# A 5x5 convolution inside a four-layer network on one Trainium2 core: shared sums seeded by a copy in PSUM instead of by identity products

## The chip, the cores and the metric

The kernel runs on one core of one Trainium2 chip, all in float32. The metric is the device time of one execution in microseconds (us). Before the change it is 4425.42 us, the median of three runs (4424.64 to 4433.18). The engines are named as in the profile: PE (TensorE, matrix products; PEld is its weight load), DVE (VectorE), ACT (ScalarE), POOL (GpSimd) and SP (SyncE, which issues DMAs).

## The reference, cut to what matters

Four images `x[4, 128, 64, 64]` go through four residual layers, each fed by a group norm. Layer 1 is the one that the change touches:

```python
x = x + attention(_gn(x))                              # layer 0, 4096 x 4096 scores per image
x = x + conv5x5(_gn(x), c)                             # layer 1: c[128, 128, 5, 5], padding 2
x = x + project(selective_scan(expand(_gn(x))))        # layer 2: two directions, 64 states
x = x + conv3x3(_gn(x), main_w)                        # layer 3
```

The convolution takes five kernel rows w0 to w4. For a pair of output rows, with image rows x0 to x5 above each other, the kernel writes

    even row = [(w1+w2)x2 + (w3+w4)x4] + w0 x0 + w1(x1-x2) + w3(x3-x4)
    odd row  = [(w1+w2)x2 + (w3+w4)x4] + w0 x1 + w2(x3-x2) + w4(x5-x4)

so that the bracket is computed once for both. Each term is five products, one for each kernel column. In the code `SUM12` and `SUM34` are w1+w2 and w3+w4, and `diff` holds the differences of rows.

## The kernel before

**Two streams.** `scan_core` (L1190) is layer 2's scan. It is written as 1024 ticks, 256 per image. A tick is one product `db` on POOL (`drive`, L1255), exponentials `da` on ACT (`decay`, L1240), the scan itself on DVE (`recur`, L1260, line L1268), a product with `cr` on DVE (L1271) or on POOL (`weigh`, L1286, line L1289), and every fourth tick a group of sums `y` on PE (`collect`, L1291, line L1309). Everything else of all images (attention, convolutions, operands of the next scan) is a second stream, `images()`, written as one generator that yields a cost in us after each piece it has issued. The loop at the end of `program` mixes them: after each half tick it adds `pace / 2` to a credit and pulls pieces from the generator until the credit is used up. `PACE` (2.8) is the credit per tick while images 0 to 2 are scanned, `ENDPACE` (1.5) while image 3 is. `PRODUCT` (0.86) is the charge for one matrix product of 512 columns, `HOP` (1.7) and `SLOT` (0.7) are charges for steps that put little on PE. This mixing fixes the order of instructions in every engine's queue; each engine then works through its queue in order.

**Stages.** While image b is scanned, the second stream does the attention of image b+1 (`attention`, L437: scores L482, exponentials L488, values L494), then its 5x5 convolution (`conv_pairs`, L830), then the operands of its scan (`scan_prep`, L1006). `before(b)` (in `program`) lets a scan begin when its operands are there; if they are not, it pulls pieces without any tick beside them. Attention keeps a second bank for scores, so the scan's `da` tiles are 512 wide; during a convolution, and all through the last image's scan, `widen` makes them 1024 wide ("wide").

**The 5x5 convolution of images 1 to 3** (`lean`) works on pairs of output rows, one even and one odd, in four chunks of 16 rows. For a chunk it makes three sums in three PSUM banks:

- `pq` in bank `s`: 10 products, the part that the two rows of each pair have in common;
- `pe0` in bank `a`: 15 products, the even rows' own part;
- `pe1` in bank `z`: 15 products, the odd rows' own part.

ACT copies `pq` to an SBUF tile `q` (L977). Then one more product with the identity matrix adds `q` to `pe0`, and another adds it to `pe1` (L991). `add` (L930) lets DVE add each finished sum to the image `xs` (L932), and ACT squares the result for the next group norm (L331). A finished sum's reader is issued late, after the third product of the following sum, so that PE's queue runs ahead. The first image has another form (`wide` weights, no identity products).

```python
if lean:
    nc.tensor.matmul(acc, ident, qs, start=False, stop=True)   # L991
    yield PRODUCT
```

Of the kernel before, what the change touches and what calls it, by code (L numbers as in the profile page):

```python
# [35 lines left out]
CH = 1024  # L36
# [6 lines left out]

PRODUCT, HOP, SLOT, PACE, ENDPACE, AHEAD = 0.86, 1.7, 0.7, 2.8, 1.5, 4


BQ, BK, BX, BP, CONVB, BD, DSKIP, MAINB, CONVW, ALOG = 0, 1, 2, 3, 4, 5, 6, 7, 8, 12
# [3 lines left out]
def conv_preact_kernel(  # L53
# [16 lines left out]
    nc = tc.nc  # L70
    B, C, H, W = x.shape
    L = H * W
# [21 lines left out]
    def bank(tag, name):  # L94
        return pools.get(tag, ps).tile([P, MM], F32, tag=tag, name=name)
# [20 lines left out]
    ident = const.tile([P, P], F32, name="ident")  # L116
# [19 lines left out]
    for d in range(2):  # L136
        r = slice(d * HALF, (d + 1) * HALF)
# [84 lines left out]
    SUM12, SUM34, HSUM, HDIF = 5, 6, 7, 8  # L222
# [607 lines left out]
    def conv_pairs(b, xs, tag, st, st2, lean):  # L830

        NP, CK = H // 2, CH // W // 2
# [33 lines left out]

        wide = pools.get("fill") if not lean else None
# [6 lines left out]
        def combine(j, n):  # L874
            for m, (p, q, op) in enumerate(
                ((1, 2, ALU.add), (0, 2, ALU.subtract), (3, 1, ALU.subtract))
            ):
                a, b_ = (rows[:, 2 * j + r : 2 * (j + n) + r - 1 : 2, :] for r in (p, q))
                nc.vector.tensor_tensor(views[m][0][:, j : j + n, :], a, b_, op)

        def differences(i):
            last = i == 3
            if wide:
                combine(8 * i, 8)
            odd(8 * i, 8 + last)
            even(8 * i + 1, 8 + last)
# [25 lines left out]
        def flat(t):  # L912
            return t.rearrange("p (h w) -> p h w", w=W)
# [3 lines left out]
        piece(1)  # L917
        differences(0)
        K5 = 5
        steps, done = [], None  # L920
        taps5 = more[0] if wide else exchange(b)[:, : NTAP * C].rearrange("p (k c) -> p k c", c=C)

        def matrix(w, dx):
            if w < SUM12:
                return taps5[:, w * K5 + dx, :]
            if w < HSUM:
                return cs[:, (w - SUM12) * K5 + dx, :]
            return more[1][:, w - HSUM, dx, :]

        def add(c, y, acc):  # L930
            i = 2 * c + y
            nc.vector.scalar_tensor_tensor(  # L932
                chunk(xs, c, y), flat(acc), 1.0, chunk(xs, c, y), ALU.mult, ALU.add,
                accum_out=st2.sum(i),
            )
            st2.squares(i, chunk(xs, c, y), xs[:, 0:1])

        for c in range(L // CH):
            j = c * CK
            if c < 2:  # L940
                piece(2 + c)
            if c < 3:
                differences(c + 1)
            accs = [
                (bank("s", f"pq_{b}_{c}"), ((SUM12, image, 2 * j + 2), (SUM34, image, 2 * j + 4))),
                (bank("a", f"pe0_{b}_{c}"),
                 ((0, image, 2 * j), (1, diff, j), (3, diff, j + 1))),
                (bank("z", f"pe1_{b}_{c}"),
                 ((0, image, 2 * j + 1), (2, diff, NP + j + 1), (4, diff, NP + j + 2))),
            ]  # L950
            if wide:
                total, first, last = (combo(n) for n in range(3))
                accs = [
                    (accs[0][0], (accs[0][1][1], (HSUM, total, j))),
                    (bank("y", f"pm_{b}_{c}"), ((HDIF, diff, j),)),
                    (accs[1][0], ((0, first, j), (3, diff, j + 1))),
                    (accs[2][0], ((2, last, j), (4, diff, NP + j + 2))),
                ]
            for n, (acc, parts) in enumerate(accs):
                k, total = 0, len(parts) * K5  # L960
                for w, view, r in parts:
                    for dx in range(K5):
                        k += 1
                        nc.tensor.matmul(  # L964
                            flat(acc), matrix(w, dx), view(r, dx),
                            start=k == 1, stop=k == total and (n == 0 or not lean),
                        )
                        if k == 3 and done is not None:
                            done()
                            done = None  # L970
                        if k % 3 == 0:
                            yield 3 * PRODUCT
                if n == 0:
                    qs = pools["bg"].tile([P, MM], F32, tag="w", bufs=4, name=f"q_{b}_{c}")

                    def done(acc=acc, qs=qs, c=c):
                        nc.scalar.copy(qs, acc)  # L977
                        for y in range(0 if lean else 2):
                            nc.gpsimd.tensor_tensor(
                                chunk(xs, c, y), chunk(xs, c, y), flat(qs), ALU.add  # L980
                            )
                    yield PRODUCT
                elif wide and n == 1:
                    def done(acc=acc, c=c):
                        for y, op in enumerate((ALU.subtract, ALU.add)):
                            nc.vector.tensor_tensor(
                                chunk(xs, c, y), chunk(xs, c, y), flat(acc), op
                            )
                else:
                    if lean:  # L990
                        nc.tensor.matmul(acc, ident, qs, start=False, stop=True)  # L991
                        yield PRODUCT

                    def done(acc=acc, c=c, y=n - len(accs) + 2):
                        add(c, y, acc)
        yield HOP
# [657 lines left out]
```

## Time and profile before

| what | value |
|---|---|
| median of three runs | 4425.42 us |
| span of the profiled execution | 4424.0 us |
| PE busy in it | 3917.4 us, 89% |
| DVE busy | 3698.5 us, 84% |
| POOL busy | 3602.1 us, 81% |
| ACT busy | 2358.3 us, 53% |
| products with the identity (L991) | 48 matrix instructions (24 products of two each), 25.1 us |
| copies of `pq` (L977) | 16 (4 of them for image 0), 585 ns each |

The span runs from the first to the last instruction of one profiled execution; it lies 1.4 us under the median and 0.6 us under the lowest of the three runs. A float32 product of 128x128 by 128x512 shows as two matrix instructions. A row "engine line op out<-in xcount | busy, mean ns | idle" is a group of alike instructions; the idle column is the time the engine stood still just before them. In a table by stretches each engine has its busy time and, in brackets, its number of instructions. Busy times of PE have modelled ends; the start times in the timeline are recorded.

Landmarks of the second stream in this execution, read from PE's timeline:

| image | attention, first query product to last product of its last block | 5x5 convolution, first to last product |
|---|---|---|
| 1 | 728.2 to 1375.6 | 1383.3 to 1558.7 |
| 2 | 1660.9 to 2309.4 | 2318.4 to 2493.9 |
| 3 | 2605.8 to 3249.4 | 3261.1 to 3436.3 |

### The profile page before, as it was taken

To read this page: it belongs to the slowest core of one execution; us is meant where nothing else is said; L and a number is where in the kernel's file an instruction comes from. 1 tells how busy PE (TensorE), PEld (TensorE's weight loads), DVE (VectorE), ACT (ScalarE), POOL (GpSimd) and SP (SyncE) were. 2 spreads that over 40 slices of the span, in tenths; PEclk is the share of its full clock that TensorE was granted. 3 is DMA by queue.
4 is the path that set the end of the run, shared out by engine and by line. 5 is a ranking of instruction groups with operands and counts; after the bars stand their busy time and mean duration, and the time that the engine had idled before them with its cause. 6 is when DMAs were issued, how large, how long until landed. Compare 5 with 4: busy or idle time off the path is not lost. (4 is left out here: it accounts for less than half of the span.)

```text
span 4424.0 us, 43050 instructions
## 1 busy us (share of the span) xinstructions
PE 3917.4 (89%) x13480; PEld 1485.9 (34%) x13480; DVE 3698.5 (84%) x3472; ACT 2358.3 (53%) x4269; POOL 3602.1 (81%) x1713
## 2 busy tenths in 40 slices
PE   8999997999999979999989889999989748575667
PEld 4444433333333323333333333333333212121212
DVE  4722217999999989999999889999999899999996
ACT  3333217666665376666664576666653744454533
POOL 3433307999999978999999889999989889999995
PEclk9999999999999989999999989999999869787888
DMA  1000016545455566554544564454545665656562
GB/s 64 21 1 1 0 53 228 182 170 175 168 186 180 179 214 212 177 175 174 180 164 180 205 231 177 165 179 173 180 175 182 226 228 193 232 202 235 187 226 84
DMA packets 213167, 726.06 MB, mean 164 GB/s; under 512 B 25152, under 2 KB 26432, under 8 KB 212672
## 3 DMA queue, kind: packets, MB, share of 16 engines
q1 hardware_dynamic: 211328, 722.49, 46.3%
q8 instruction: 108, 1.77, 0.2%
q14 instruction: 131, 1.07, 0.1%
q10 hardware_dynamic: 1600, 0.73, 0.1%
HBM read 653.98 MB, written 69.14 MB: 163 GB/s over the span
## 5 line engine op out<-in xcount | busy, mean ns | idle before, releaser
L1258 POOL TENSOR_TENSOR db<-dx,br 128x1024 f32<-128x1024 f32 x1024 | 2398.1, 2365 | 223.8 <-DMA dx<-dxd 55.6
L1251 ACT ACTIVATE da<-de,a_neg 128x512 f32<-128x512 f32 (+1 forms) x1640 | 1302.4, 797 | 740.6 <-DVE da L1268 300.5
L482 PE MATMUL sc<-r,x 128*128 128x512 f32 x2048 | 1078.6, 609 | 14.8 <-ACT last L1284 6.9
L494 PE MATMUL acc<-exchange,v 128*128 128x512 f32 x2048 | 1048.3, 594 | 2.3
L1289 POOL TENSOR_TENSOR hc<-hc,cr 128x1024 f32<-128x1024 f32 x386 | 913.0, 2365 | 22.5 <-ACT last L1284 19.7
L1271 DVE TENSOR_TENSOR hc<-da,cr 128x512 f32<-128x512 f32 (+1 forms) x1003 | 839.6, 837 | 65.0 <-DVE da L1268 0.5
L1268 DVE TENSOR_TENSOR_SCAN da<-da,last,db 128x512 f32<-128x512 f32 (+1 forms) x480 | 863.1, 1798 | 24.3 <-POOL db L1258 12.1
L488 ACT ACTIVATE exchange<-sc 128x512 f32<-128x512 f32 x1024 | 603.5, 589 | 510.4 <-PE sc L482 503.9
L1309 PE MATMUL y<-hc,sel 128*32 128x512 f32 x4096 | 611.9, 647 | 270.6 <-POOL hc L1289 245.3
L482 PEld LDWEIGHTS sc<-r,x 128*128 128x128 f32 x2048 | 361.3, 190 | 585.6 <-issue 379.2
L494 PEld LDWEIGHTS acc<-exchange,v 128*128 128x128 f32 x2048 | 386.4, 190 | 499.2 <-issue 478.0
L1268 DVE TENSOR_TENSOR_SCAN hc<-da,last,db 128x512 f32<-128x512 f32 (+1 forms) x288 | 490.9, 1704 | 6.5 <-ACT da L1251 5.2
L1268 DVE TENSOR_TENSOR_SCAN da<-da,da,db 128x512 f32<-128x512 f32 x365 | 469.7, 1287 | 6.2 <-ACT da L1251 5.9
L536 POOL TENSOR_TENSOR sidep<-sidep,exchange 128x512 f32<-128x512 f32 x120 | 170.7, 1422 | 273.5 <-ACT exchange L488 271.3
L1268 DVE TENSOR_TENSOR_SCAN hc<-da,hc,db 128x512 f32<-128x512 f32 x251 | 322.0, 1283 | 35.6 <-ACT da L1251 11.8
L1309 PEld LDWEIGHTS y<-hc,sel 128*32 128x32 f32 x4096 | 114.4, 113 | 706.1 <-POOL hc L1289 337.7
L536 DVE TENSOR_TENSOR sided<-sided,exchange 128x512 f32<-128x512 f32 x120 | 95.9, 799 | 221.5 <-ACT exchange L488 220.1
L1268 DVE TENSOR_TENSOR_SCAN da<-da,db 128x512 f32<-128x512 f32 (+1 forms) x158 | 232.5, 1471 | 15.5 <-POOL db L1258 7.1
L698 PE MATMUL pcm<-xpm,cs 128*128 128x512 f32 x432 | 210.1, 635 | 23.1 <-ACT xpm L387 23.1
L964 PE MATMUL pe<-df,exchange 128*128 128x512 f32 x480 | 214.2, 595 | 0.0
L516 PE MATMUL zp<-exchange,ones 128*32 128x512 f32 x1536 | 204.9, 600 | 8.3 <-DVE xs L583 8.3
L1284 ACT COPY last<-da 128x1 f32<-128x1 f32 x474 | 73.8, 156 | 254.5 <-DVE hc L1271 252.0
(241 smaller groups left out, 2839.1 us busy)
## 6 DMA issues: line engine op xcount, KB each, us to landing
br<-bm SPq DMA_DIRECT2D x512, 512.0 KB, 5.2
cr<-cm SPq DMA_DIRECT2D x512, 512.0 KB, 3.9
de<-dd SPq DMA_DIRECT2D x64, 512.0 KB, 4.7
dx<-dxd SPq DMA_DIRECT2D x64, 512.0 KB, 6.2
x<-in_x_dram SPq DMA_DIRECT2D x16, 512.0 KB, 5.9
xs<-in_x_dram SPq DMA_DIRECT2D x16, 512.0 KB, 6.1
xsd<-xs SPq DMA_DIRECT2D x16, 512.0 KB, 6.0
xcd<-xc SPq DMA_DIRECT2D x16, 512.0 KB, 2.8
```

The costliest lines, as they stand in the source:

```text
L482: nc.tensor.matmul(sc, xn[:, bass.ts(j, P)], rq[blk], start=True, stop=True)
L488: nc.scalar.activation(pt, sc, AF.Exp)
L494: nc.tensor.matmul(acc[blk], v[:, j, :], ring[:, u % NRING, :], start=j == 0, stop=j == NJT - 1)
L536: eng.tensor_tensor(s, s, ring[:, u % NRING, :], ALU.add)
L698: nc.tensor.matmul(acc.rearrange("p (r w) -> p r w", w=W), weights[:, t, :], xp[:, y : y + RPM, dx : dx + W], start=t == 0, stop=t == k * ...
L964: nc.tensor.matmul(flat(acc), matrix(w, dx), view(r, dx), start=k == 1, stop=k == total and (n == 0 or not lean),)
L1251: nc.scalar.activation(da, rep["de", b, c, d, g][:, bass.ts(h, size)], AF.Exp, scale=a_neg[:, at(i)])
L1258: nc.gpsimd.tensor_tensor(dbs[i], rep["dx", b, c, d, g], rows["b", b, c, d, q], ALU.mult)
L1268: nc.vector.tensor_tensor_scan(h, da, db[:, cut], before, ALU.mult, ALU.add)
L1271: nc.vector.tensor_tensor(hc[:, cut], h, rows["c", b, c, d, q][:, cut], ALU.mult)
L1289: nc.gpsimd.tensor_tensor(hcs[i], hcs[i], rows["c", b, c, d, q], ALU.mult)
L1309: nc.tensor.matmul(y[r : r + SG, :], sel, hcs[first + gg][:, bass.ts(h, MM)], start=q == back, stop=False, tile_position=(0, r), skip_grou ...
```

## The change

For images 1 to 3 the common sum of a chunk goes into a bank that is `s` and `z` in turn. ACT copies it into bank `a`. The even rows' 15 products then add to that copy, and the odd rows' 15 products add to the common sum in its own bank; neither begins with `start=True`, so they add to what stands there. The tile `q` and the 24 identity products are gone. The order of a chunk's sums becomes: common sum of chunk c, odd rows of chunk c-1, even rows of chunk c. For the first chunk nothing lies between the common sum and the even rows, and a `yield HOP` stands there. `PACE` goes from 2.8 to 2.77. The charge for the identity products falls away, and with it the one `PRODUCT` that was charged after the common sum. The first image's convolution keeps its order.

```diff
-PRODUCT, HOP, SLOT, PACE, ENDPACE, AHEAD = 0.86, 1.7, 0.7, 2.8, 1.5, 4
+PRODUCT, HOP, SLOT, PACE, ENDPACE, AHEAD = 0.86, 1.7, 0.7, 2.77, 1.5, 4
...
+        def group(acc, parts, begun=False):
+            nonlocal done
+            k, of_all = 0, len(parts) * K5
+            for w, view, r in parts:
+                for dx in range(K5):
+                    k += 1
+                    nc.tensor.matmul(
+                        flat(acc), matrix(w, dx), view(r, dx),
+                        start=k == 1 and not begun, stop=k == of_all, skip_group_check=lean,
+                    )
+                    if k == 3 and done is not None:
+                        done()
+                        done = None
+                    if k % 3 == 0:
+                        yield 3 * PRODUCT
+
+        NCK, held, owns = L // CH, {}, {}
+
+        def shared_of(c):
+            j = c * CK
+            held[c] = bank("sz"[c % 2], f"pq_{b}_{c}")
+            yield from group(
+                held[c], ((SUM12, image, 2 * j + 2), (SUM34, image, 2 * j + 4))
+            )
+
+        def second_of(c):
+            nonlocal done
+            j, acc = c * CK, held.pop(c)
+            yield from group(
+                acc, ((0, image, 2 * j + 1), (2, diff, NP + j + 1), (4, diff, NP + j + 2)), True
+            )
+            done = lambda: add(c, 1, acc)
+
+        def first_of(c):
+            nonlocal done
+            j, acc = c * CK, owns.pop(c)
+            yield from group(
+                acc, ((0, image, 2 * j), (1, diff, j), (3, diff, j + 1)), True
+            )
+            done = lambda: add(c, 0, acc)
+
+        def part(c):
+            owns[c] = bank("a", f"pe0_{b}_{c}")
+            nc.scalar.copy(owns[c], held[c])
+
+        for c in range(NCK + 1 if lean else 0):
+            if c < NCK:
+                advance(c)
+                yield from shared_of(c)
+                done = lambda c=c: part(c)
+            if c > 0:
+                yield from second_of(c - 1)
+            else:
+                yield HOP
+                done()
+                done = None
+            if c < NCK:
+                yield from first_of(c)
...
-                    if lean:
-                        nc.tensor.matmul(acc, ident, qs, start=False, stop=True)
-                        yield PRODUCT
```

More of the change, by code (lines that the diff above doesn't have):

```diff
@@ L919, in conv_pairs @@
         K5 = 5
-        steps, done = [], None
+        done = None
         taps5 = more[0] if wide else exchange(b)[:, : NTAP * C].rearrange("p (k c) -> p k c", c=C)
@@ L936, in add, with advance @@
             st2.squares(i, chunk(xs, c, y), xs[:, 0:1])
-        for c in range(L // CH):
-            j = c * CK
+        def advance(c):
             if c < 2:
@@ L943, in conv_pairs @@
                 differences(c + 1)
-            accs = [
[L945 to L949, printed above, removed]
-            ]
[L951 to L958, printed above, removed]
@@ L959, in conv_pairs @@
-            for n, (acc, parts) in enumerate(accs):
[L960 to L972, printed above, removed]
+        def group(acc, parts, begun=False):
[13 more added lines that the diff above has]
+                        yield 3 * PRODUCT
@@ new lines, in first_of @@
+        def first_of(c):
[18 more added lines that the diff above has]
+                done()
+                done = None
+            if c < NCK:
+                yield from first_of(c)
@@ new lines, in conv_pairs @@
+        for c in range(0 if lean else NCK):
+            j = c * CK
+            advance(c)
+            total, first, last = (combo(n) for n in range(3))
+            accs = [
+                (bank("s", f"pq_{b}_{c}"), ((SUM34, image, 2 * j + 4), (HSUM, total, j))),
+                (bank("y", f"pm_{b}_{c}"), ((HDIF, diff, j),)),
+                (bank("a", f"pe0_{b}_{c}"), ((0, first, j), (3, diff, j + 1))),
+                (bank("z", f"pe1_{b}_{c}"), ((2, last, j), (4, diff, NP + j + 2))),
+            ]
+            for n, (acc, parts) in enumerate(accs):
+                yield from group(acc, parts)
@@ L977, in done @@
                         nc.scalar.copy(qs, acc)
-                        for y in range(0 if lean else 2):
+                        for y in range(2):
                             nc.gpsimd.tensor_tensor(
@@ L982, in conv_pairs @@
                     yield PRODUCT
-                elif wide and n == 1:
+                elif n == 1:
                     def done(acc=acc, c=c):
```

## The prediction

> **What bounds the kernel now.** I read the table by stretches first, because the share over the whole span mixes stages. Columns: stretch, its length, then busy us of PE, PEld, DVE, ACT, POOL, the granted clock, DMA share and GB/s.
>
> ```profile
> 800.00:1370.00 570.00, 561.67 (x2170) 210.87 (x2172) 541.58 (x558) 368.16 (x758) 531.77 (x230) 1.00 0.51 178
> 1700.00:2300.00 600.00, 590.71 (x2266) 219.18 (x2258) 570.34 (x586) 385.44 (x795) 561.45 (x243) 1.00 0.50 174
> 2640.00:3245.00 605.00, 599.62 (x2312) 222.37 (x2311) 576.80 (x592) 390.49 (x806) 565.91 (x245) 1.00 0.50 175
> 1396.00:1540.00 144.00, 144.00 (x449) 57.27 (x450) 135.55 (x84) 56.73 (x63) 136.75 (x62) 1.00 0.53 181
> 2330.00:2478.00 148.00, 148.00 (x472) 58.10 (x471) 137.61 (x85) 56.74 (x63) 142.06 (x64) 1.00 0.49 178
> 3273.00:3434.00 161.00, 161.00 (x513) 63.28 (x512) 150.34 (x94) 61.80 (x69) 153.19 (x69) 1.00 0.50 176
> 3600.00:4350.00 750.00, 497.48 (x1560) 148.92 (x1556) 727.87 (x430) 360.09 (x570) 724.54 (x331) 0.81 0.61 213
> ```
>
> The first three rows lie in the attentions of images 1 to 3, the next three in their 5x5 convolutions, the last in the scan of image 3. In the convolutions PE is busy all the time, at full clock, and the list of PE's waits in 1396 to 1540 is empty: there PE sets the pace, with DVE and POOL at 93 to 96%. In the attentions PE is at 98.7% (1752.0 of 1775 us), DVE at 95.1%, POOL at 93.5%: three engines near their limit. At the end PE has a third of its time free, and DVE and POOL set the pace.
>
> The same table for the products `db` alone counts ticks, one each: 164, 174 and 175 in the attentions, 44, 45 and 49 in the convolutions, 235 in the last stretch. So a tick takes 1775/513 = 3.46 us in an attention, 453/138 = 3.28 in a convolution, 750/235 = 3.19 at the end.
>
> Then PE's timeline of the convolution (start, length, with modelled end, so I use starts):
>
> ```profile
> 1409.83 1.92 PE L1309 MATMUL y<-hc,sel 128*32 128x512 f32 x16
> 1411.68 1.12 PE L991 MATMUL pe<-q,ident 128*128 128x512 f32 x2
> 1412.64 4.50 PE L964 MATMUL pe<-xpe,exchange 128*128 128x512 f32 x10
> 1416.98 6.17 PE L964 MATMUL pe<-df,exchange 128*128 128x512 f32 x14
> 1423.08 1.92 PE L1309 MATMUL y<-hc,sel 128*32 128x512 f32 x16
> 1424.93 2.84 PE L964 MATMUL pe<-df,exchange 128*128 128x512 f32 x6
> 1427.62 1.02 PE L991 MATMUL pe<-q,ident 128*128 128x512 f32 x2
> 1428.47 4.06 PE L964 MATMUL pq<-xpe,cs 128*128 128x512 f32 x9
> ```
>
> An identity product holds PE's queue for 1428.47 - 1427.62 = 0.85 us (0.96 right after sums `y`). Sums `y` of four ticks hold it for 1.85 us, which is 0.46 us a tick, and 0.49 with the `skip` products once in 32 ticks.
>
> **The change, part by part.**
>
> *Identity products.* 2 for each of 4 chunks of 3 images, 24 x 0.855 = 20.5 us of PE, all in stretches where PE is the limit: **-20.5 us**.
>
> *Where the ticks go.* The scan has 1024 ticks before and after, and no edit takes DVE or POOL work out of a tick, so what counts is which ticks lie beside which work. The planner's credit can be followed in both sources. Attentions end at ticks 190, 444 and 700 before, and at 192, 446 and 701 after; convolutions end at 243, 497, 753 against 243, 496, 752; the operands of images 2 and 3 are finished one tick earlier. So attentions get 184 ticks each before and 186 after (+6 in all, at `PACE` 2.77 instead of 2.8), convolutions 53 each before and 51, 50, 51 after (-7), the operand stages 17, 19 and 20 both times, and the end 251 before and 252 after (+1).
>
> - A tick less in a convolution saves only its share of `y`, as PE is the limit there: 7 x 0.49 = **-3.4 us**. A convolution's products per tick rise slightly, because 39 charges now stand for 40 products of a chunk; DVE (423.5/138 = 3.07 us a tick) and POOL (3.13) stay under PE's 3.28.
> - A tick more at the end costs a whole one: **+3.2 us**.
> - A tick more in an attention, with the same attention products spread over more ticks, is the disputed cost. If PE alone set the pace there, it would cost 0.49 us; if DVE and POOL did, 3.46. Six ticks: +2.9 or +20.8 us. The waits speak for neither: in the third attention DVE waited for the exponentials and for `db` as listed below, 7.5 of 605 us, and PE's idle time there is 5.4 us.
>
> ```profile
> DVE da L1268 <- ACT da L1251: 4.9, 8, 2.2
> DVE hc L1268 <- ACT da L1251: 1.7, 4, 0.8
> DVE da L1268 <- POOL db L1258: 0.9, 3, 0.4
> ```
>
> Both engines hardly wait, so I take the middle: **+11.9 us**. I keep both ends for the range.
>
> *The copy.* 12 copies from PSUM to SBUF become 12 from PSUM to PSUM. The page's rows bracket the new form: exponentials without bias take 589 ns into SBUF (L488) and 600 into PSUM (L1127), activations with bias 686 (L1098) and 667 (L1099), and L977 itself 585. So it is 585 give or take 20 ns; ACT has over half its time free in the convolution.
>
> The Trainium skill, "ScalarE: Activation LUTs", in "Step-by-step: what each stage is for", calls ScalarE's way into PSUM faster than into SBUF; the exponential's rows here say 11 ns slower and the biased ones 19 ns faster. By either, the sum moves by less than 0.1 us.
>
> *Waits that the copy adds.* For chunks 1 to 3 the copy is issued three products into the odd rows' sum of the chunk before, and PE first needs it 12 products later: 12 x 0.86 = 10.3 us of cover. Bank `a` must also have been read by DVE, which is issued ten products before the copy. Of the 12 copies before, nine start 0.03 to 0.04 us after the last product of `pq` ends and the others 0.2, 1.8 and 2.5 us after, behind exponentials that wait for DVE. So I cost these at nothing; if the cover went, nine even-row sums would wait, with `y` queued behind them on PE and the scan's tiles behind `y`. For chunk 0 there is no cover: PE goes from the common sum to the even rows and must wait for the end of the last product (0.16 us after its slot), a hop of 0.04, the copy of 0.585 and a hop back of about 0.05, some 0.85 us. Three images: **+2.6 us**. The odd rows' sum follows 15 products after ACT has read its bank, and the banks `s` and `z` are reused 12 products after their reader is issued: nothing.
>
> *Not on the path.* SP's queue, the DMAs, POOL's instructions and DVE's additions are the same in number; `q` leaves a ring of four tiles for which nobody waits in a convolution.
>
> The Trainium skill, "PSUM — Partial Sum Buffer", in "The four PSUM rules" and its summary, speaks against the change: engine writes do not touch the bits that decide whether a product adds or overwrites, so a seed other than zero should go through PE. It also says that products add where an earlier product set the bit, which bank `a` has had since the attention. No row here shows a product adding to a copy. Kept to the letter, the rule brings 12 identity products back, 10.3 us of the 20.5.
>
> *Sum.* -20.5 - 3.4 + 2.6 + 3.2 + 11.9 = **-6.2 us**. The profiled span, 4424.0, becomes 4417.8; it lies 1.4 us under the median of 4425.4, which becomes **4419.2**. What a measurement of this kernel can tell from no change is about 0.2%, 8.85 us.
>
> **Rivals.**
>
> - *PE alone sets the pace of the attentions.* For it: PE is the busiest at 98.7%. Against it: its loads of weights and ends are modelled, and DVE waits for it little. Six ticks cost 2.9 us: -20.5 - 3.4 + 2.6 + 3.2 + 2.9 = -15.2, **4410**. This is what the lower pace is worth if it is right.
> - *DVE and POOL set it alone.* For it: DVE's waits are 1% too, and its small gaps between instructions count as idle though they can't be used. Six ticks cost 20.8: +2.7, **4428**. The gain of the convolution is given back tick by tick.
> - *The seed is late in every chunk* (the other side). Place: the even rows' first product in chunks 1 to 3, nine times. ACT's queue is in order, and a copy behind an exponential that waits for DVE (2.4 us is a usual such wait in the convolution) also delays the next exponentials. It costs from the point where a copy ends more than 10.3 us after its issue; at 2.4 us each, 9 x 2.4 = +21.6, so +15.4 on the forecast, **4441**. It makes the kernel slower by over 0.2% from 1.7 us each. Against it: the latest copy of before ended 3.1 us after its sum.
> - *The identity products are not gone, or come back as others*: excluded, the instruction order of the changed kernel has none in images 1 to 3.
>
> **How the numbers follow.** Forecast 0.40, PE alone 0.28, DVE and POOL alone 0.20, late seeds 0.08, anything else 0.04, counted as slower. The operand stages give noise: with 0.03 less credit per tick their pieces fall otherwise between ticks, and the pieces pulled without a tick before scans 1, 2 and 3 go from 16, 2 and 2 to 18, 0 and 0. An operand stage of image 1 (102 us for about 60 pieces) is 1.7 us a piece, so two pieces either way are 3.4 us. The range goes from the first rival less that (4406) to the second plus that, with some of the late seeds (4433). Faster by over 0.2% (under 4416.6) are the first rival and 0.06 of the forecast, 0.34; within 0.2%: the rest of the forecast, 0.34, and 0.19 of the second rival, 0.53; slower the late seeds, 0.01 of the second rival and 0.04 of the rest, 0.13.
>
> **What the profile after would show.** Right if: the convolutions (175.5, 175.5 and 175.2 us from first to last product) shrink to about 168 each, with PE's list of waits empty but for one of some 0.85 us ahead of the first even-row sum; the attentions (647.4, 648.5, 643.6 us) grow by about 4 us each, the tick falling from 3.46 to about 3.445. Growth of 1 us, and 3.43, means PE set their pace; growth of 7 us at 3.46 means DVE and POOL did. Late seeds would show as PE waiting for ACT's copy twelve times. The forecast is wrong if the convolutions don't shrink by 7 us, if DVE or POOL turns out to be their limit, or if the operand stages move by over 4 us.

## The result, and the profile after

The changed kernel takes 4439.88 us (median of 15 runs, 4435.58 to 4446.72) against 4425.81 us for the kernel before (15 runs). The ratio is 1.0029, 95% interval 1.0022 to 1.0036: slower, where 4419.2 was forecast, and outside the range. The profiled execution has a span of 4438.5 us against 4424.0, 14.5 us more.

The table by stretches of the changed kernel comes first, with the same columns as the one of before (stretch, length, busy us of PE, PEld, DVE, ACT and POOL, clock, DMA share, GB/s): three attentions, three convolutions, the last stretch.

```profile
800.00:1370.00 570.00, 560.81 (x2153) 207.45 (x2151) 543.07 (x559) 367.14 (x758) 533.49 (x230) 1.00 0.52 178
1700.00:2300.00 600.00, 589.91 (x2263) 219.17 (x2260) 569.57 (x586) 385.04 (x796) 561.65 (x242) 1.00 0.50 173
2640.00:3240.00 600.00, 591.78 (x2285) 219.66 (x2284) 573.52 (x590) 388.09 (x801) 565.90 (x245) 1.00 0.51 176
1410.00:1550.00 140.00, 140.00 (x443) 55.13 (x445) 130.54 (x82) 54.00 (x61) 132.94 (x61) 1.00 0.51 179
2340.00:2490.00 150.00, 148.83 (x473) 58.42 (x472) 140.59 (x88) 57.49 (x66) 144.55 (x66) 1.00 0.49 176
3275.00:3425.00 150.00, 149.34 (x474) 58.49 (x473) 137.29 (x87) 57.31 (x65) 140.89 (x64) 1.00 0.52 176
3600.00:4360.00 760.00, 495.16 (x1544) 150.38 (x1544) 725.49 (x428) 358.26 (x567) 720.62 (x329) 0.80 0.61 210
```

In the attentions the picture is that of before: PE 98.4%, DVE 95.3%, POOL 93.8%, and one tick (one product `db`, counted in the same stretches) takes 1770/512 = 3.457 us where it took 3.46. The lower pace bought no shorter tick. In the convolutions PE is still full. The last row covers as many ticks as before (234 against 235) in 10 us more, with no engine busier. Over the whole of the three attentions POOL begins 562 products `db` where it began 555.

The waits of DVE in the third attention, which before were 4.9, 1.7 and 0.9 us, are as small as then:

```profile
DVE da L1306 <- ACT da L1289: 3.0, 2, 1.6
DVE da L1306 <- POOL db L1296: 2.0, 2, 1.6
```

The stages, read from PE's timeline, say where the 14.5 us came from ("operands" is the time from the end of a convolution to the next image's first query product, for image 3 to the first product `po`; the last stretch runs from there to the end):

| us | before | after | difference | predicted |
|---|---|---|---|---|
| start to attention 1, with image 0's own stages | 728.2 | 731.5 | +3.3 | 0 |
| attentions 1 / 2 / 3 | 647.4 / 648.5 / 643.6 | 652.4 / 654.0 / 652.7 | +19.6 | +11.9 |
| from attention to convolution, all three | 28.3 | 30.9 | +2.6 | 0 |
| convolutions 1 / 2 / 3 | 175.5 / 175.5 / 175.2 | 167.8 / 167.9 / 167.7 | -22.8 | -21.3 |
| operands 1 / 2 / 3 | 102.2 / 111.9 / 154.3 | 105.2 / 102.4 / 158.2 | -2.6 | 0, give or take 3.4 |
| last stretch | 833.4 | 847.7 | +14.3 | +3.2 |

The edited code did what was forecast. PE's timeline at the start of the first such convolution (start, length, idle before and its releaser in brackets):

```profile
1402.00 6.32 PE L950 MATMUL pq<-xpe,cs 128*128 128x512 f32 x14
1408.98 4.59 PE L950 MATMUL pe<-xpe,exchange 128*128 128x512 f32 x10 [0.66 <-ACT pe L987]
1413.41 1.02 PE L950 MATMUL pe<-df,exchange 128*128 128x512 f32 x2
...
1428.59 6.32 PE L950 MATMUL pq<-xpe,cs 128*128 128x512 f32 x14
1434.74 4.49 PE L950 MATMUL pq<-xpe,exchange 128*128 128x512 f32 x10
```

A row `pq<-xpe,cs` is a common sum, `pe` are the even rows, and `pq<-xpe,exchange` are odd rows, which add in the common sum's own bank. The common sum is followed by the even rows after 0.66 us in the first chunk, and in the second by the odd rows of the chunk before with no gap. PE's waits list this once for each image, 0.7, 1.2 and 0.7 us, against 0.85 forecast. No other seed is late. The loss lies in code that the change doesn't touch: the attentions and the last stretch.

### The profile page after: what moved, and what is told of

It is laid out like the page before. It is cut to its first block, busy times and chain, and to the rows that moved or that the text cites. A ratio compares the mean times of both kernels' runs of the same rounds, so it can differ in the third digit from the quotient of the medians.

```text
span 4438.5 us, 42967 instructions
## 1 busy us (share of the span) xinstructions
PE 3902.2 (88%) x13432; PEld 1481.5 (33%) x13432; DVE 3691.0 (83%) x3475; ACT 2358.7 (53%) x4275; POOL 3610.7 (81%) x1717
## 5 line engine op out<-in xcount | busy, mean ns | idle before, releaser
L1327 POOL TENSOR_TENSOR hc<-hc,cr 128x1024 f32<-128x1024 f32 x390 | 922.7, 2366 | 16.7 <-ACT last L1322 14.9
L1306 DVE TENSOR_TENSOR_SCAN da<-da,last,db 128x512 f32<-128x512 f32 (+1 forms) x476 | 851.7, 1789 | 37.8 <-POOL db L1296 22.5
L1347 PE MATMUL y<-hc,sel 128*32 128x512 f32 x4096 | 598.7, 643 | 289.0 <-POOL hc L1327 277.3
L1306 DVE TENSOR_TENSOR_SCAN da<-da,da,db 128x512 f32<-128x512 f32 x366 | 471.0, 1287 | 10.8 <-ACT da L1289 10.3
L536 POOL TENSOR_TENSOR sidep<-sidep,exchange 128x512 f32<-128x512 f32 x120 | 170.7, 1422 | 273.5 <-ACT exchange L488 271.3
L950 PE MATMUL pq<-xpe,cs 128*128 128x512 f32 x280 | 134.0, 630 | 36.0 <-ACT xpe L387 36.0
```

The lines of the kernel that those rows point to most:

```text
L536: eng.tensor_tensor(s, s, ring[:, u % NRING, :], ALU.add)
L1306: nc.vector.tensor_tensor_scan(h, da, db[:, cut], before, ALU.mult, ALU.add)
L1327: nc.gpsimd.tensor_tensor(hcs[i], hcs[i], rows["c", b, c, d, q], ALU.mult)
L1347: nc.tensor.matmul(y[r : r + SG, :], sel, hcs[first + gg][:, bass.ts(h, MM)], start=q == back, stop=False, tile_position=(0, r), skip_grou ...
```

## The experiments

One theory and its rivals were stated. **A:** the convolution's gain is real, and it is lost in two places, by the ticks that the lower pace and the missing charges moved into the attentions (where DVE and POOL set the tick, so that each costs some 3.3 us), and by the shift of one tick between the two streams in the last stretch. **Rivals:** PE sets the pace of the attentions and something else costs the time there; the new form itself disturbs other engines; or (D) DVE and POOL are at their limit in the convolutions as well, so that PE's saving can't be turned into time at all.

The kernel before was run again beside each group of kernels, with medians of 4428.12 to 4430.0 us. The ratios below are to those runs; between groups, compare ratios and not microseconds.

### The form alone, and the pace alone

`old_charges` is the changed kernel with the charges and the pace of before, so that each tick lies beside the same work as before:

```diff
-PRODUCT, HOP, SLOT, PACE, ENDPACE, AHEAD = 0.86, 1.7, 0.7, 2.77, 1.5, 4
+PRODUCT, HOP, SLOT, PACE, ENDPACE, AHEAD = 0.86, 1.7, 0.7, 2.8, 1.5, 4
...
                 done = lambda c=c: part(c)
+                yield PRODUCT
             if c > 0:
                 yield from second_of(c - 1)
+                yield PRODUCT
             else:
-                yield HOP
+                yield 0.0
...
                 yield from first_of(c)
+                yield PRODUCT
```

> The changed convolution with the charges and the pace of before, so that every piece of the second stream falls on the same tick as in the kernel before (attentions end at ticks 190, 444 and 700, convolutions at 243, 497 and 753, the 3x3 convolutions begin at 802, 878 and 954). Theory A (the change lost by moving ticks: whole ticks into the attentions, and the last image's second stream one tick earlier): the convolutions take about 169 us instead of 175.4, attentions and last stretch stay as before, 3 x 6 = 18 us less, 4408. Theory B (the seeded sums themselves disturb what follows, wherever the ticks lie): attentions some 5 us longer each and the last stretch some 14 us longer as in the changed kernel, 4430 or more.

`pace_alone` is the kernel before with `PACE` 2.77 and nothing else.

> The kernel before with the pace 2.77 alone. Attentions get 186 ticks, and the operands come late: 42, 20 and 10 pieces are pulled without a tick before scans 1, 2 and 3 instead of 16, 2 and 2; the 3x3 convolutions begin at the ticks of before (802, 878, 954). Theory A: attentions 5 to 7 us longer each, convolutions as before at 175, 52 pieces more at rest at 1 to 1.7 us, less what they no longer take beside ticks, last stretch as before at 833: 4440 to 4470. Theory B: attentions as before, since the seeded sums aren't there, 4430 or less.

Measured: `old_charges` 4424.69 us, ratio 0.999 (0.9981 to 0.9999); `pace_alone` 4439.65, ratio 1.0027 (1.0018 to 1.0036). So the form alone is a gain of some 4 us, not 20: neither theory A's 4408 us nor theory B came true, as attentions (1938.0 us in all) and last stretch (834.6) stayed as before, which speaks against the new form disturbing other stages. The pace alone is as slow as the whole change. In `pace_alone` the attentions take 651.9, 652.8 and 650.0 us, +15.2 in all, though the convolution is the old one.

Where the form's gain goes is seen in the convolutions, 176 us from the first product of before. First the kernel before, then `old_charges`, the same three stretches:

```profile
1383.00:1559.00 176.00, 175.48 (x552) 68.73 (x552) 164.70 (x101) 71.15 (x80) 168.75 (x78) 0.99 0.49 169
2318.00:2494.00 176.00, 175.60 (x556) 68.91 (x560) 162.82 (x101) 70.41 (x81) 166.73 (x77) 0.99 0.48 176
3261.00:3437.00 176.00, 175.85 (x560) 68.99 (x564) 163.15 (x101) 70.77 (x82) 168.19 (x78) 0.99 0.51 178
```

```profile
1383.00:1559.00 176.00, 169.62 (x536) 66.00 (x536) 166.35 (x105) 70.84 (x79) 171.00 (x79) 0.98 0.50 173
2318.00:2494.00 176.00, 171.60 (x551) 65.53 (x549) 164.01 (x100) 70.95 (x80) 167.47 (x77) 0.99 0.51 181
3261.00:3437.00 176.00, 169.56 (x549) 65.04 (x547) 164.95 (x104) 68.71 (x78) 168.42 (x77) 0.99 0.52 182
```

PE gets 16 us of idle time in the three, and POOL works only 3 us more in the same time. Before, POOL was busy 168.75 us of the first and waited 6.7 us for one load of `br`: 175.4 of 176 us. PE was full there, and so was POOL, if the wait is counted. In the other two POOL was busy 166.7 and 168.2 us and waited 6.1 and 6.6 us for loads. With the identity products gone, the convolutions' last products come 7.0, 3.6 and 4.3 us sooner and the operand stages behind them take 5.4, 1.6 and 4.5 us longer, since the same ticks remain to be done. Of 14.9 us some 3 are left by the last stretch. This speaks for D.

### Both engines, or POOL alone?

If POOL alone held the convolutions, giving part of its work to DVE should free the gain. In three kernels POOL takes the product with `cr` on every fourth tick of a convolution instead of every third:

```diff
-                    i % 3 == 2 if "wide" in pools
+                    i % 4 == 3 if "convolving" in ready and "wide" in pools
+                    else i % 3 == 2 if "wide" in pools
```

`before_pool4` is the kernel before with it, `old_charges_pool4` the one above, `after_late_pool4` the kernel `after_late` of the section on the shift below. `before_new_ticks`, run beside them, is the old form with its identity products on the changed kernel's ticks (pace 2.77, no charges for the identity products, the last stretch on the ticks of before).

> The kernel before, with POOL taking the product with cr in every fourth tick of a convolution instead of every third (DVE takes the others); all ticks as before. Theory A: PE alone is left as the limit of the convolutions, so they stay at 175 and the total within 3 us of before; POOL shows 4% more idle time there. Rival C (POOL is the only limit of the convolutions): 53 ticks x 0.2 us = 10 us less each, 4395. Rival D (DVE is the limit): 5 us longer each, 4440.

> The seeded sums with the charges and ticks of before, and POOL taking the product with cr in every fourth tick of a convolution. Theory A: with both limits eased the saving of PE can be had: convolution and operand stage together 5 to 6 us shorter per image than before, where old_charges gained only 1 to 1.5; total 4407 to 4412 where before is 4426. Rival D (DVE, at 93% in the convolutions, is the limit next to PE): 5 us more DVE work each undo it, 4425 or more.

> The changed kernel with the last stretch on the ticks of before, and POOL taking the product with cr in every fourth tick of a convolution. Theory A: at 51 ticks the convolutions are bound by PE (167.8 busy of 168), so easing POOL gains little, 0 to 2 us each; total 4421 to 4428. The attentions keep their 6 ticks more. Rival C (POOL is still the limit at 51 ticks): 8 us less each, 4404.

> The convolution of before, identity products and all, on the ticks of the changed kernel (pace 2.77, the identity products and the last common product not charged, last stretch on tick 802). It differs from after_late in the form of the sums alone. Theory A (the saving in PE counts only where the convolutions also get fewer ticks, since POOL has none to spare at 53): with 51, 50 and 51 ticks POOL needs about 168 us a convolution, but PE still about 174: convolutions 174 to 175 instead of 168, 6 us each longer than in after_late, about 18 us slower than that, 4444 where before is 4426. Rival C (the convolutions are bound by the scan alone, PE's products don't count): 168 as in after_late, same time as it.

Measured: 4433.82 (ratio 1.0011, 1.0002 to 1.002), 4436.68 (1.0015, 1.0006 to 1.0024), 4437.72 (1.002, 1.0011 to 1.0029). All three are slower than the kernel without the edit, and the convolutions are no shorter (`old_charges_pool4`: 167.7, 172.6 and 170.7 us, where `old_charges` has 168.5, 171.9 and 170.9). POOL alone, which I had come to think, falls. In the same stretches (the third cut at 3436) POOL's busy time drops from 505.9 us in `old_charges` to 474.8 in `old_charges_pool4`, and DVE's rises from 494.3 to 501.3 of 527: this fits DVE as the next limit, which no kernel tested by itself. Of that kernel's 12 us more, 5.9 lie in the operand stages, 4.3 in the attentions and 2.5 in the last stretch, by one profile each. `before_new_ticks` takes 4449.03 (1.0044, 1.003 to 1.0057); its convolutions take 175.8, 174.4 and 173.8 us, with seven ticks fewer beside them in all: there PE is the limit. The same ticks with the new form (`after_late`, below) take 4428.72. So the new form is worth some 20 us where ticks have been moved out of the convolutions and 4 where they have not.

### Who sets the tick in an attention

`light_values` is the kernel before without about every second product with the values in the attentions of images 1 to 3 (120 products for each image, some 103 us of PE; that part of the attention is left out). `light_scan` is the kernel before without the products with `cr` in the ticks beside attentions, so that DVE and POOL have less to do there (that part of the scan is left out).

```diff
-                    values(w)
+                    if b == 0 or w % 2 == 0 or w % NJT == NJT - 1:
+                        values(w)
```

```diff
+                if "wide" not in pools and "operands" not in ready:
+                    bare.add(i)
+                    pooled[i] = True
...
-            if to_pool(i):
+            if to_pool(i) and i not in bare:
```

> The kernel before without every second values product (attention weights times v) in images 1 to 3, charges and ticks unchanged: it leaves out 15 of 32 values products in each block, 120 per image, 103 us of PE per image. Theory A (DVE and POOL set the tick of an attention, each tick costs them 3.4 us whatever PE does): attentions 0 to 15 us shorter each, 630 to 647 us, tick 3.40 to 3.46, total down by at most 45. Theory F (PE sets it, as in my first rival): attentions 70 us shorter or more each, down to DVE's 3.3 us a tick, 575 or less; in between means both share it.

> The kernel before without the product with cr in the ticks of the attentions of images 1 to 3, on DVE as on POOL: it leaves out that product there, 0.83 us of DVE and 0.95 us of POOL per tick. PE's work, charges and ticks are unchanged. Theory A: the tick falls from 3.46 to what PE needs, which by its issue times is about 3.40: attentions 8 to 13 us shorter each, so both limits lie within 2% of each other and neither alone is worth more. Theory F (PE far under the tick): attentions 30 us or more shorter. If they don't shrink at all, PE alone sets the tick.

`light_values`, three stretches of the attentions:

```profile
800.00:1370.00 570.00, 503.20 (x1949) 171.59 (x1945) 542.26 (x559) 366.83 (x760) 532.70 (x230) 0.96 0.52 178
1700.00:2300.00 600.00, 522.81 (x2064) 177.35 (x2056) 573.65 (x591) 387.37 (x804) 565.95 (x244) 0.98 0.50 174
2640.00:3230.00 590.00, 522.96 (x2017) 180.51 (x2015) 563.59 (x581) 380.45 (x790) 553.46 (x239) 0.96 0.51 175
```

`light_scan`, stretches that end with its shorter attentions:

```profile
800.00:1360.00 560.00, 559.31 (x2174) 211.41 (x2176) 417.15 (x365) 359.38 (x760) 385.73 (x166) 1.00 0.50 175
1700.00:2280.00 580.00, 579.17 (x2251) 217.09 (x2244) 430.56 (x373) 370.82 (x784) 398.67 (x170) 1.00 0.50 175
2640.00:3210.00 570.00, 569.17 (x2210) 212.97 (x2209) 422.28 (x367) 364.09 (x771) 389.80 (x167) 1.00 0.50 176
```

Without 310 us of products PE is at 88%, and the attentions take 646.4, 643.2 and 639.0 us: 1.0, 5.3 and 4.6 us less. The whole takes 4424.07, ratio 0.9988 (0.9979 to 0.9997). DVE and POOL, at 95 and 94% as ever, keep the time: a tick takes 1760/510 = 3.45 us. With DVE at 74% and POOL at 69% PE is busy 99.9% of the time and a tick takes 1710/501 = 3.41 us; the attentions take 632.3, 636.0 and 635.2: 15.1, 12.5 and 8.4 us less; the whole 4390.74, ratio 0.9915 (0.9899 to 0.993). So DVE and POOL together set the tick, and PE stands 1.3 to 2.3% behind them. They were eased together, so which of the two it is was not separated. The 5% of the time that DVE isn't busy was no reserve: with PE eased, the tick hardly fell from 3.46.

The Trainium skill, "Perfetto Trace Analysis", section "Identifying the Most-Contended Engine", names the engine with the highest busy share as the one to improve, and adds that the busy share of matmuls is not a good measure for TensorE. These runs bear out the second half: PE had the highest share, 98.7%, and with 310 us of its work gone, 16% of the attentions' 1939.5 us, they became 10.9 us or 0.6% shorter.

### One tick of shift in the last stretch

Image b's last layer begins in the second stream by credit, not by tick. In the changed kernel the charges of a convolution are 8.6 us less for each image (12 charges of 0.86 are gone and one `HOP` of 1.7 is new) and the credit is 7.7 us less, and after three images the second stream stands one tick earlier. The products `db` (POOL's timeline) of ticks 802, 806, 864, 929 and 1023 start at 3637.8, 3653.6, 3839.0, 4050.0 and 4349.3 us before, and at 3637.9, 3661.6, 3849.4, 4062.9 and 4362.9 after: level up to tick 802, then late by 8.0, 10.4, 12.9 and 13.6 us. `before_early` puts the kernel before one tick earlier by smaller charges for the four loads with which image 0's last layer begins (4 x 0.375 is 1.5, the credit of one tick there), `after_late` the changed kernel one tick later:

```diff
-                    yield HOP
+                    yield HOP - 0.375 if b == 0 else HOP      # before_early
+                    yield HOP + 0.375 if b == 0 else HOP      # after_late
```

> The kernel before, with 1.5 us less charged in the loading of image 0's rows for the last layer, so that all of the second stream behind image 3's operands falls one tick earlier (3x3 convolutions begin at ticks 801, 877 and 953, as in the changed kernel). Nothing else differs, up to the first product po the time is that of before. Theory A: the first 3x3 products stand ahead of the sums y of tick 802 in PE's queue, ynd's store is late and holds br's loads on SP's queue, POOL waits some 8 us for br near 3650; the stretch from the first po to the end takes about 847 us instead of 833, 4438. Theory B: no change within noise, 4426.

> The changed kernel, with 1.5 us more charged in the loading of image 0's rows for the last layer, so that the second stream behind image 3's operands falls on the ticks of before (802, 878, 954). Theory A: the wait of some 8 us for br near 3660 is gone and the stretch from the first po to the end takes about 833 us as before, 4426 in all; what the convolutions save and what the attentions lose cancel. Theory B: as the changed kernel, 4440.

Measured: `before_early` 4439.43, ratio 1.002 (1.0011 to 1.0029), last stretch 846.9; `after_late` 4428.72, ratio 0.9996 (0.9987 to 1.0005), last stretch 834.5. Either way the shift is worth some 13 us of the stretch, whatever form the convolution has. `after_late` still has the longer attentions (652.9, 655.4, 652.5), so its time is the change's without this second loss.

What the shift does is read from POOL's waits in 3590 to 4350 (in total, how often, longest), before and then after:

```profile
POOL db L1258 <- DMA dx<-dxd: 7.3, 4, 3.6
POOL db L1258 <- DMA br<-bm: 5.2, 9, 1.0
```

```profile
POOL db L1296 <- DMA br<-bm: 16.8, 7, 8.1
POOL db L1296 <- DMA dx<-dxd: 13.9, 6, 5.2
```

12.5 us of waits for loads have become 30.7. The longest can be followed on three engines. PE after, and then before:

```profile
3645.53 5.49 PE L698 MATMUL pcm<-xpm,cs 128*128 128x512 f32 x6 [16.64 <-ACT xpm L387]
3650.95 2.06 PE L1347 MATMUL y<-hc,sel 128*32 128x512 f32 x16
3652.94 1.08 PE L1358 MATMUL y<-xcr,skip 128*64 128x512 f32 x4
```

```profile
3635.62 3.63 PE L1309 MATMUL y<-hc,sel 128*32 128x512 f32 x14 [4.71 <-POOL hc L1289]
3639.19 1.28 PE L1320 MATMUL y<-xcr,skip 128*64 128x512 f32 x4
3650.08 6.14 PE L698 MATMUL pcm<-xpm,cs 128*128 128x512 f32 x10 [9.61 <-ACT xpm L387]
```

SP's queue of DMA issues after, and then before:

```profile
3637.34 0.51 SPq L1272 DMA_DIRECT2D cr<-cm  x1
3654.68 1.13 SPq L1375 DMA_DIRECT2D ynd<-ys  x2
3655.90 2.12 SPq L1272 DMA_DIRECT2D br<-bm  x1
```

```profile
3637.16 0.51 SPq L1234 DMA_DIRECT2D cr<-cm  x1
3644.71 1.13 SPq L1337 DMA_DIRECT2D ynd<-ys  x2
3645.93 0.57 SPq L1234 DMA_DIRECT2D br<-bm  x1
```

The first products of the 3x3 convolution now stand ahead of the sums `y` in PE's queue. They wait for `xpm` until 3645.5, and `y` with them. ACT copies `y` to `ys` at 3654.1 instead of 3644.1; the store of `ys` waits for that on SP, from 3637 to 3654.7, and the next load of `br` behind it goes out at 3655.9 instead of 3645.9. POOL stands still for 8.12 us, until 3661.6. This accounts for the first 8.0 us; the 5.6 us lost behind tick 806 were not followed in the same way.

### The stores off SP's queue

`after_ys_act` and `old_charges_ys_act` issue the store of `ys` from ACT. Four more kernels issue the stores of the output rows from ACT as well: `after_stores_act`, `before_early_stores_act`, `before_stores_act` and `old_charges_stores_act`.

```diff
-                nc.sync.dma_start(ynds[b][m][r, :], ys[r, :])
+                nc.scalar.dma_start(ynds[b][m][r, :], ys[r, :])
...
-                nc.sync.dma_start(of[b][:, cut], to)          # the four more
+                nc.scalar.dma_start(of[b][:, cut], to)
```

> The changed kernel, ticks and all (3x3 convolutions at 801, 877 and 953), with the store of the scan's sums (ynd from ys) issued from ACT's queue instead of SP's, so that a late ys no longer holds the loads of br and cr that stand behind it on SP. Theory A (the last stretch's 14 us come from that place in SP's queue): ys is copied as late as before the edit, but POOL's wait of 8 us for br near 3660 is gone and the stretch from the first po to the end takes 833 to 838 us instead of 848; total 4425 to 4432. Theory E (the loss is PE's or ACT's own lateness, not SP's queue): stretch 847, total 4438 to 4440.

> The seeded sums with the charges and ticks of before, and the ynd store on ACT's queue. Theory A: the ticks of before have no late ys to speak of, so 0 to 5 us better than old_charges (4 us under before), 4418 to 4425 where before is 4426. Theory E: as old_charges.

> The changed kernel with two stores moved from SP's queue to ACT's: the scan's sums (ynd<-ys) and the output rows (out_dram<-o). Its last stretch, from the last scan's first po to the span's end, was 847.7 us. Theory A (the 14 us that the last stretch lost are waits of POOL for br, dx and de loads that stand behind these stores on SP): 833 to 838, all four waits of 2.7 to 8.1 us at ticks 806, 864, 929 and 992 gone, total 4425 to 4430. Theory E (the order of the 3x3 convolution's pieces against the ticks costs it on PE, ACT or DVE, and SP's queue only shows it): 843 to 847, total 4434 to 4438.

> The kernel before, with the last stretch one tick early, and the two stores on ACT's queue. Its last stretch was 846.9 us. Theory A: 833 to 838, total 4424 to 4429. Theory E: 843 to 847, total 4434 to 4438.

> The kernel before with the two stores on ACT's queue; its last stretch was 833.4 us, with 12.5 us of waits of POOL for loads. Theory A: 825 to 834, within 4 us of before_early_stores_act, since one tick more or less no longer matters; total 4417 to 4426. Theory E: 830 to 836, 8 us or more under before_early_stores_act.

> The new convolution with the charges and the pace of before, and the two stores on ACT's queue. Its last stretch was 834.7 us. Theory A: 825 to 834, total 4414 to 4423. Theory E: 832 to 837, total 4420 to 4425.

Measured (ratios to the kernel before, with 95% intervals; the last stretch is from the profile):

| stores of `ys` and output rows | SP, SP | ACT, SP | ACT, ACT |
|---|---|---|---|
| changed kernel: us | 4439.88 | 4436.85 | 4433.09 |
| ratio | 1.0029 (1.0022 to 1.0036) | 1.0014 (1.0005 to 1.0023) | 1.0006 (0.9997 to 1.0016) |
| last stretch | 847.7 | 844.5 | 841.1 |
| `old_charges`: us | 4424.69 | 4426.48 | 4426.99 |
| ratio | 0.999 (0.9981 to 0.9999) | 0.9994 (0.9985 to 1.0003) | 0.9997 (0.9988 to 1.0006) |
| last stretch | 834.7 | 835.7 | 836.7 |
| `before_early`: us | 4439.43 | | 4440.31 |
| ratio | 1.002 (1.0011 to 1.0029) | | 1.0026 (1.0016 to 1.0036) |
| last stretch | 846.9 | | 838.4 |
| kernel before: us | 4425.81 | | 4436.64 |
| ratio | 1 | | 1.0017 (1.0008 to 1.0026) |
| last stretch | 833.4 | | 838.2 |

One store moved takes the wait of 8.1 us away, but only 3.2 us of the stretch: in `after_ys_act` tick 806 starts at 3652.9 us, 0.7 ahead of the kernel before, and tick 1023 at 4359.6, 10.3 behind it, so most of what the wait cost is lost again later. With both moved, the shift costs the old form 0.2 us of the stretch instead of 13.5, and the new form 4.4 instead of 13.0. In `before_early_stores_act` hardly a wait for `br` is left, while those for `dx` stay:

```profile
POOL db L1258 <- DMA dx<-dxd: 11.7, 6, 5.3
...
POOL db L1258 <- DMA br<-bm: 0.8, 1, 0.8
```

With both stores moved, POOL's waits for loads in that window are 12.5 us in `before_early_stores_act` (30.2 in `before_early`) and 12.3 in `after_stores_act` (30.7 in the changed kernel), and the stretches shrink by 8.5 and 6.6 us. So half of the shift's price or somewhat more goes through the loads that stand behind these stores on SP, by these profiles; the rest stays open. Only 838.4 comes near theory A's 833 to 838 for the shifted kernels; 841.1 and 844.5 lie between the two theories, nearer to E. The gain that was hoped for did not come either: with both stores on ACT's queue the stretch is 836.7 to 841.1 in all four, where the kernels without the shift were expected at 825 to 834, and the kernel before becomes 0.17% slower. What the stores cost on ACT's queue was not taken apart. By whole times the shift still costs the old form 0.0009 (1.0026 against 1.0017, intervals that overlap) where it cost 0.002; its one profiled execution, at 4435.26 us, was 5 us under its median, so the 838.4 flatters it. Whole times show no gain at all from the move for `before_early` (1.0026 against 1.002).

## Why the prediction was wrong, step by step

- *Identity products and the copy*: right. The convolutions shrank by 7.6 us each (about 168 was written down), the one uncovered seed wait is 0.7 to 1.2 us, and the rival of late seeds in every chunk didn't happen. The copy into PSUM has a median of 570 ns against 586 into SBUF, inside the bounds taken.

```profile
L987 ACT COPY pe<-pq x12: 538/570/592, 1408.4 to 3384.7; 128x512 f32<-128x512 f32 x12
```

  (Durations in ns: least, median, most.) The Trainium skill, "PSUM — Partial Sum Buffer", in "The four PSUM rules", has two halves here: an engine's write leaves the adding bits alone, and a product adds where an earlier product set the bit. The changed kernel rests on the second half, since bank `a` was written by products all through the attention. Kept to the first alone, it would have had 12 identity products and 10.3 us back; at equal ticks the runs show the form without any identity products at some 20 us less, about the price of all 24.

- *"Both engines hardly wait, so I take the middle: +11.9"*: this step failed. Six more ticks in the attentions cost 19.6 us, 3.3 each, near the upper end (20.8) and the second rival. (By the 562 products `db` against 555 it is seven ticks and 2.8 each; the other kernels at the new pace lie between +14.4, `after_ys_act`, and +26.2, `after_late_pool4`, all over the middle that I took.) I read small waits of DVE as no evidence. The better reading was in the same rows: DVE at 95% and POOL at 93.5% of the time in all three attentions, with a tick of 3.46 us that a lower pace did not shorten. A look at waits can't tell three engines near their limit apart; taking work away can.

- *"A tick less in a convolution saves only its share of `y`"* and *DVE and POOL "stay under PE's 3.28"*: the sum came out (-22.8 against -21.3), the reading behind it failed. In the convolutions too DVE and POOL together were at their limit: with the ticks where they were, the same edit shortens the kernel by 4 us (`old_charges`). The 20 us of PE could only be had by moving ticks out, and every tick moved cost close to its full price in an attention. The 1024 ticks are the work that has to be done, and no stage tried has room in which they are cheap. I counted a tick's price in two different currencies, PE's in one stage and a mean in the other.

- *"A tick more at the end costs a whole one: +3.2"*: this step failed as well, and no rival held what happened. The last stretch lost 14.3 us, in code that the diff doesn't touch, because of the shift by one tick: undone, the stretch is back at 834.5 (`after_late`). It put products that wait ahead of the sums, a store that waits ahead of loads, and POOL behind the loads; that chain is shown for the first 8 us, and what holds the rest stays open. I had worked out that the operands of images 2 and 3 end one tick earlier, and priced it as a tick; I didn't ask what is issued next to what after the shift. Had I listed SP's queue around tick 802, where the last scan's sums and the first 3x3 convolution meet, the store of `ys` ahead of `br` would have stood there.

- *The operand stages* moved by -2.6 us in all, inside the 3.4 allowed, but that is luck: single ones moved by 3.0, -9.5 and 3.9, and over 4 us was named as a sign of being wrong. Nor is the -9.5 of image 2 noise: that stage takes 101.4 to 104.3 us in every profile at pace 2.77 and 110.2 to 116.3 in every one at 2.8. The wait from attention to convolution (+2.6) was not foreseen; ahead of image 1 it is 10.3 us in every profile at the new pace and 7.6 at the old, and why stays open. Image 0's part (+3.3) differs from one execution to the next: the attention there takes 472.2 or 473.8 us in kernels with the same code for it, and `after_stores_act`, which has the changed kernel's code and pace up to there, begins attention 1 at 728.3 as before.

The measured time comes near the 4441 of the late seeds by coincidence: no seed was late but the three foreseen. (The +15.4 of that rival counts from the kernel before, not from the forecast.)

With the two failed steps replaced, the forecast's own sum gives -21.3 + 19.6 + 14.3 = +12.6 us; the measured 14.1 of the medians (14.5 of the profiles) is that and the small rest.

Of the versions that leave nothing out, the new form with the old charges is the fastest by its median: 4424.69 us, ratio 0.999 (0.9981 to 0.9999). The intervals of `after_late` and of the two kernels that move its stores overlap with it.

## What to carry to other kernels

Where two instruction streams are interleaved by a budget, an edit of the budget is an edit of every stage: price the ticks that it moves by the stage that receives them, and take the price from the stream that has to be finished, not from the busiest engine. An engine at 98% is not shown to be the limit while two others stand at 95%: take work from each in turn (here from PE, and from DVE and POOL together) and see what gives time back. And after any shift of order, list what stands ahead of the loads in the queue that issues them, above all stores that wait for an engine.

## What the runs showed of the hardware

- SP issues its DMAs in order: one store that waited for a copy on ACT held the load behind it back: it was issued at 3655.9 us, and at 3648.8 with the store on another queue (`after_stores_act`).
- Which engine issues a store matters in both directions: on ACT's queue the same two stores took 6.6 us off the shifted stretch (847.7 to 841.1) and put 4.8 us on the unshifted one (833.4 to 838.2), by one profile each; the unshifted whole became 0.17% slower.
- With PE at 88% instead of 99% in the attentions its granted clock there fell to 0.96 to 0.98 (`light_values`), where it was 1.00.
- POOL's product `db` takes the same time whether DVE is at 95% or at 74%: a median of 2362 ns in the first attention before and 2357 ns in `light_scan`.
